# Splitting the tail of one store per block into 120 rows and 8 rows

## The chip, the cores and the metric

The kernel runs on one core of a Trainium2 chip. The metric is the device time of one execution in microseconds (us); a time is the median of several runs. Inside the core, TensorE (PE) multiplies matrices and writes to PSUM, VectorE (DVE), ScalarE (ACT) and GpSimd (POOL) work elementwise, and SyncE (SP) only issues transfers. Sixteen DMA engines move data between SBUF, the core's working memory of 128 partitions ("rows" below), and DRAM.

## The reference

The input is x with B = 4096 samples, F = 32 fields and D = 64 numbers per field, and one 64x64 matrix W[p] for each of the P = 32*31/2 = 496 pairs of fields (i, j) with i < j:

```python
idx_i, idx_j = np.triu_indices(F, k=1)
vi = inputs[:, idx_i, :]
vj = inputs[:, idx_j, :]
vidots = jnp.einsum('bpd,pde->bpe', vi, W)
return vidots * vj          # (4096, 496, 64) float32
```

The output has 4096*496*64 floats, 520 MB. All is float32. One pair of one sample is 64 floats, 256 bytes.

## The kernel before

A block is 256 samples: two tiles (`kt` = 0, 1) of 128 samples, one sample per partition. The 16 blocks are worked one after the other, and in each tile the 496 pairs go in five groups with 90, 106, 90, 105 and 105 pairs. A group fills one output buffer `ot` and leaves with one store, so there are ten stores in a block and 160 in all. Three `ot` buffers take turns.

```python
P = 128
NB = 2
groups = [(0, 3), (3, 7), (7, 11), (11, 17), (17, F - 1)]
cap = max(p0[b] - p0[a] for a, b in groups)
...
opool = ctx.enter_context(tc.tile_pool(name="opool", bufs=3))
psum = ctx.enter_context(tc.tile_pool(name="psum", bufs=4, space=bass.MemoryType.PSUM))
...
# the matrices W, 128 pairs to a load (112 in the last), one pair's 16 KB to a partition
nc.sync.dma_start(out=raw[c][: b - a, :], in_=wflat[a:b])
...
for s in range(NBLK * NB * NS):
    ...                                  # x of the next block is loaded from ACT's queue
    if pa == base:
        ot = opool.tile([P, cap, D], F32, tag="ot", name=f"ot_{t}_{g}")
    ...                                  # matmuls: x_i^T W into ps, up to 16 pairs
    if i in aside and c0 == 0:
        nc.scalar.copy(tmp, src)         # PSUM to SBUF
        nc.gpsimd.tensor_mul(dst, tmp, xj)
    else:
        nc.vector.tensor_mul(dst, src, xj)
    if pa + m == end:
        nc.sync.dma_start(
            out=rows_of(out, blk).rearrange("(p k) n d -> p k n d", k=NB)[:, kt, base:end, :],
            in_=ot[:, : end - base, :],
        )
```

Each store reads 128 rows of `ot`. A row is one piece of 90, 105 or 106 pairs, that is 23,040, 26,880 or 27,136 bytes without a gap, both in SBUF and in DRAM.

Of the kernel before, what the change touches and what calls it, by code (L numbers as in the profile page):

```python
# [12 lines left out]
def kernel(  # L13
# [16 lines left out]
    nc = tc.nc  # L30

    B, F, D = x.shape
    P = 128
    NB = 2
# [11 lines left out]
    cap = max(p0[b] - p0[a] for a, b in groups)  # L46

    aside = (1, 3, 5, 7, 9, 11, 13)

    cuts = [*range(0, NP, P), NP]  # L50
    wrows = list(zip(cuts[:-1], cuts[1:]))
# [13 lines left out]
    def rows_of(dram: bass.AP, blk: int) -> bass.AP:  # L65
        return dram[blk * NB * P : (blk + 1) * NB * P]

    def new_x(blk: int):

        xs[blk] = xpool.tile([P, 1 + NB * F, D], F32, tag="xs", name=f"xs_{blk}")  # L70
        nc.gpsimd.memset(xs[blk][:, 0, :], 0.0)  # L71

    def load_x(blk: int, eng, k0: int = 0, k1: int = NB):
        src = rows_of(x, blk).rearrange("(p k) f d -> p (k f) d", k=NB)
        eng.dma_start(out=xs[blk][:, 1 + k0 * F : 1 + k1 * F, :], in_=src[:, k0 * F : k1 * F, :])
# [7 lines left out]
    def load_w(c: int):  # L83

        a, b = wrows[c]
        pool, tag = ((opool, "ot"), (xpool, "xs"), (const, "w3"), (xpool, "xs"))[c]
        raw[c] = pool.tile([P, D * D], F32, tag=tag, name=f"raw_{c}")
        nc.sync.dma_start(out=raw[c][: b - a, :], in_=wflat[a:b])

    def order_w(c: int, k: int, copy):  # L90
        r = wrows[c][1] - wrows[c][0]
        rp = tpool.tile([P, EU, 2, D], F32, tag="tmp", name=f"rp_{c}_{k}")
        src = raw[c][:r, :].rearrange("p (d h e) -> p e h d", h=2, d=D)
        copy(rp[:r], src[:, k * EU : (k + 1) * EU])  # L94
        return rp

    def turn_w(c: int, k: int, rp, copy):
        r = wrows[c][1] - wrows[c][0]
        if c not in wT:
            wT[c] = const.tile([P, r, E2], F32, tag=f"w{c}", name=f"wT_{c}")  # L100
        pt = psum.tile([P, EU, P], F32, tag="ps", name=f"ptw_{c}_{k}")
        for n in range(EU):
            nc.tensor.transpose(  # L103
                pt[:, n, :r], rp[:r, n].rearrange("p h d -> p (h d)"), ident[:r, :r]
            )
        copy(wT[c][:, :, k * EU : (k + 1) * EU], pt[:, :, :r].rearrange("p e r -> p r e"))  # L106

    def turn_x(blk: int, k: int, q: int, copy):

        pt = psum.tile([P, RUN, P], F32, tag="ps", name=f"ptx_{blk}_{k}_{q}")  # L110
        for n in range(RUN):
            s = k * F + q * RUN + n
            nc.tensor.transpose(  # L113
                pt[:, n, :], xs[blk][:, s : s + 2, :].rearrange("p f d -> p (f d)"), ident
            )
        xT = xtpool.tile([P, RUN, P], F32, tag="xT", name=f"xT_{blk}_{k}_{q}")
        copy(xT, pt)  # L117
        return xT
# [32 lines left out]
    v, p, a = nc.vector.tensor_copy, nc.gpsimd.tensor_copy, nc.scalar.copy  # L151
# [10 lines left out]
    ot = None  # L162
    for s in range(NBLK * NB * NS):
        t, st = divmod(s, NS)
        blk, kt = divmod(t, NB)
        g, i, c0, m = steps[st]
        if st == LATE and kt == 0 and blk and blk + 1 < NBLK:
            new_x(blk + 1)
            load_x(blk + 1, nc.scalar)
        for what, *args in due.get(s, ()):  # L170
            if what == "x":
                xT[tuple(args)] = turn_x(*args, a)
            else:
                c, k = args
                turn_w(c, k, order_w(c, k, (v, p)[k % 2]), a)
                if k == NU - 1 and c == 1:
                    load_w(3)
                if k == NU - 1 and c == 3:
                    new_x(1)
                    load_x(1, nc.scalar)  # L180

        base, end = p0[groups[g][0]], p0[groups[g][1]]
        pa = p0[i] + c0
        if pa == base:
            ot = opool.tile([P, cap, D], F32, tag="ot", name=f"ot_{t}_{g}")
        ps = psum.tile([P, 2, CH, E2], F32, tag="ps", name=f"ps_{s}")
        for c, (lo, hi) in enumerate(wrows):
            lo, hi = max(pa, lo), min(pa + m, hi)
            if lo < hi:
                for h in range(2):  # L190
                    n = i + 1 - h
                    nc.tensor.matmul(  # L192
                        ps[:, h, lo - pa : hi - pa, :],
                        xT[blk, kt, n // RUN][h * D : (h + 1) * D, n % RUN, :],
                        wT[c][h * D : (h + 1) * D, lo - wrows[c][0] : hi - wrows[c][0], :],
                        start=True,
                        stop=True,
                    )
        o = pa - base
        j = 1 + kt * F + i + 1 + c0  # L200
        dst = ot[:, o : o + m, :].rearrange("p m (h e) -> p m h e", h=2)
        src = ps[:, :, :m, :].rearrange("p h m e -> p m h e")
        xj = xs[blk][:, j : j + m, :].rearrange("p m (h e) -> p m h e", h=2)
        if i in aside and c0 == 0:
            tmp = tpool.tile([P, CH, 2, E2], F32, tag="tmp", name=f"tmp_{s}")
            nc.scalar.copy(tmp, src)  # L206
            nc.gpsimd.tensor_mul(dst, tmp, xj)  # L207
        else:
            nc.vector.tensor_mul(dst, src, xj)  # L209
        if pa + m == end:  # L210
            nc.sync.dma_start(  # L211
                out=rows_of(out, blk).rearrange("(p k) n d -> p k n d", k=NB)[:, kt, base:end, :],
                in_=ot[:, : end - base, :],
            )


# [25 lines left out]
```

## Time and profile before

| what | value |
|---|---|
| time, median of 3 runs | 1359.63 us (1359.32 to 1359.97) |
| span of the profiled execution | 1357.5 us |
| PE busy | 1171.5 us (86%) |
| DVE busy | 951.3 us (70%) |
| POOL busy | 546.2 us (40%) |
| ACT busy | 371.1 us (27%) |
| DRAM read, written | 41.68 MB, 520.09 MB |
| mean rate of all transfers | 415 GB/s |
| from issue to landing of a store, min/median/max | 9.2/17.0/20.4 us |

Busy shares are averages over the span. In the profile's lists a group of instructions or a wait is named by its line in the kernel, its engine and the tiles that it writes and reads: `out_dram<-ot` is a store, `ps` a product in PSUM. A wait line such as "DVE ot L209 <- DMA out_dram<-ot" gives the total, the number and the longest of VectorE's waits that a landed store ended. A stage line gives a stretch of time, its length, the busy time of PE, PE's weight loads, DVE, ACT and POOL, then the granted TensorE clock, the mean busy share of the 16 DMA engines and the rate in GB/s. DMA queue lines give packets, MB and the share of 16 engines' time; q1 carries what SP issues, q10 what ACT issues, q8 and q14 fetch instructions.

### The profile page before, as it was taken

The page shows a single profiled execution, that of the slowest core. Times are in us where ns is not written, and L with a number is a line of the kernel's source. Part 1 is how long each engine was busy: PE and PEld are TensorE (multiplying, and loading weights), DVE is VectorE, ACT ScalarE, POOL GpSimd, SP SyncE. Part 2 cuts the span into 40 slices and gives each one's busy share as a digit, 9 for nine tenths or more (in the row PEclk, how much of TensorE's full clock was granted, in tenths as well). Part 3 has the DMA queues.
Part 4 walks back from the last instruction along what each step waited for, and adds up shares of the span by engine and source line. Part 5 has one row for each costly group of instructions (what it writes and reads, how often), then busy time and mean ns, then how long its engine had stood idle before and what let it go on. Part 6 is the DMA issues. An engine that isn't in the chain of part 4 may idle for free.

```text
span 1357.5 us, 17867 instructions
## 1 busy us (share of the span) xinstructions
PE 1171.5 (86%) x7424; PEld 681.2 (50%) x7424; DVE 951.3 (70%) x1259; ACT 371.1 (27%) x367; POOL 546.2 (40%) x253
## 2 busy tenths in 40 slices
PE   5998988888888888988889888899888889888894
PEld 4554554545455454554545445455454545545552
DVE  5686876767677676766667767677776777767783
ACT  3432322222222222222322222222222322223220
POOL 4544433443333443334434334433344433444441
PEclk9998998989999999998989999999898999999997
DMA  7999999999999999999999999999999999999997
GB/s 291 388 430 431 426 424 431 431 422 426 401 424 413 430 423 412 428 409 431 410 417 425 413 433 407 421 423 410 428 412 424 426 409 424 406 431 428 417 419 335
DMA packets 26128, 562.92 MB, mean 415 GB/s; under 512 B 2896, under 2 KB 2896, under 8 KB 2896
## 3 DMA queue, kind: packets, MB, share of 16 engines
q1 hardware_dynamic: 23744, 529.28, 92.0%
q10 hardware_dynamic: 2304, 32.51, 5.7%
q8 instruction: 58, 0.95, 0.3%
q14 instruction: 22, 0.18, 0.0%
HBM read 41.68 MB, written 520.09 MB: 414 GB/s over the span
## 4 chain that ended last, share of the span: by engine, by line
DMA 50%; PE 23%; DVE 18%; POOL 4%; issue 3%; ACT 0%; DVEq 0%; SPq 0%; POOLq 0%; ACTq 0%
DMA out_dram<-ot 49%; PE ps L192 19%; DVE ot L209 18%; PE ptx L113 4%; POOL ot L207 3%; DMA raw<-in_L_rec_W_dram 1%; POOL rp L94 1%; PE ptw L103 0%; ACT tmp L206 0%; DVE rp L94 0%; DVEq L209 0%; DVE xT L117 0%; ACT wT L106 0%; SPq L211 0%; POOLq L207 0%
## 5 line engine op out<-in xcount | busy, mean ns | idle before, releaser
L209 DVE TENSOR_TENSOR ot<-ps,xs 128x1024 f32<-128x1024 f32 (+15 forms) x1248 | 938.6, 807 | 378.4 <-DMA out_dram<-ot 195.3
L192 PE MATMUL ps<-wT,xT 64*128 64x512 f32 (+14 forms) x6272 | 1025.2, 467 | 118.0 <-DVE ot L209 105.5
L192 PEld LDWEIGHTS ps<-wT,xT 64*128 64x128 f32 x6272 | 554.0, 193 | 554.6 <-DVE ot L209 281.9
L207 POOL TENSOR_TENSOR ot<-tmp,xs 128x1024 f32<-128x1024 f32 x224 | 527.3, 2360 | 623.5 <-ACT tmp L206 397.7
L206 ACT COPY tmp<-ps 128x1024 f32<-128x1024 f32 x224 | 226.7, 1012 | 465.5 <-PE ps L192 460.6
L117 ACT COPY xT<-ptx 128x1024 f32<-128x1024 f32 x127 | 128.5, 1012 | 470.2 <-PE ptx L113 470.2
L113 PE MATMUL ptx<-ident,xs 128*128 128x128 f32 x1024 | 143.8, 285 | 48.9 <-DVE ot L209 34.3
L113 PEld LDWEIGHTS ptx<-ident,xs 128*128 128x128 f32 x1024 | 113.2, 144 | 95.4 <-issue 51.3
L71 POOL MEMSET xs<- 128x64 f32 x16 | 2.4, 151 | 146.7 <-DVE ot L209 146.7
L94 POOL COPY rp<-raw 128x1024 f32<-128x1024 f32 (+1 forms) x7 | 16.1, 2299 | 16.1 <-DMA raw<-in_L_rec_W_dram 11.8
L106 ACT COPY wT<-ptw 128x1024 f32<-128x1024 f32 (+1 forms) x15 | 14.7, 984 | 28.1 <-PE ptw L103 28.1
L103 PE MATMUL ptw<-ident,rp 128*128 128x128 f32 (+1 forms) x128 | 17.0, 280 | 3.2 <-DVE rp L94 2.0
L94 DVE COPY rp<-raw 128x1024 f32<-128x1024 f32 (+1 forms) x9 | 11.0, 1233 | 12.3 <-DMA raw<-in_L_rec_W_dram 11.9
L103 PEld LDWEIGHTS ptw<-ident,rp 128*128 128x128 f32 (+1 forms) x128 | 14.1, 145 | 10.2 <-issue 5.6
L106 ACT ACT_TABLE_LOAD x1 | 1.3, 1283 | 1.2 <-PEq L229 1.2
L117 DVE COPY xT<-ptx 128x1024 f32<-128x1024 f32 x1 | 1.2, 1208 | 0.0
L106 DVE COPY wT<-ptw 128x1024 f32<-128x1024 f32 x1 | 1.2, 1208 | 0.0
masks.py:197 POOL MEMSET ident<- 128x128 f32 x1 | 0.2, 205 | 0.3 <-POOLq L229 0.3
masks.py:199 POOL TENSOR_SCALAR_AFFINE_SELECT ident<-ident 128x128 f32<-128x128 f32 x1 | 0.3, 292 | 0.0
L229 POOL MEMSET const-float32-0.0<- 128x1 f32 x1 | 0.1, 98 | 0.2 <-issue 0.2
L229 POOL MEMSET const-bfloat16-1.0<- 128x1 bf16 x1 | 0.1, 101 | 0.0
L229 POOL MEMSET const-uint8-127<- 128x1 uint8 x1 | 0.1, 101 | 0.0
(1 smaller groups left out, 0.1 us busy)
## 6 DMA issues: line engine op xcount, KB each, us to landing
out_dram<-ot SPq DMA_DIRECT2D x64, 3360.0 KB, 16.2
out_dram<-ot SPq DMA_DIRECT2D x64, 2880.0 KB, 16.7
out_dram<-ot SPq DMA_DIRECT2D x32, 3392.0 KB, 17.2
xs<-in_r_inputs_dram ACTq DMA_DIRECT2D x15, 2048.0 KB, 16.6
raw<-in_L_rec_W_dram SPq DMA_DIRECT2D x3, 2048.0 KB, 15.6
raw<-in_L_rec_W_dram SPq DMA_DIRECT2D x1, 1792.0 KB, 15.7
xs<-in_r_inputs_dram ACTq DMA_DIRECT2D x1, 1024.0 KB, 11.4
xs<-in_r_inputs_dram SPq DMA_DIRECT2D x1, 1024.0 KB, 17.7
```

Source lines behind the costliest of these rows:

```text
L71: nc.gpsimd.memset(xs[blk][:, 0, :], 0.0)
L94: copy(rp[:r], src[:, k * EU : (k + 1) * EU])
L103: nc.tensor.transpose(pt[:, n, :r], rp[:r, n].rearrange("p h d -> p (h d)"), ident[:r, :r])
L106: copy(wT[c][:, :, k * EU : (k + 1) * EU], pt[:, :, :r].rearrange("p e r -> p r e"))
L113: nc.tensor.transpose(pt[:, n, :], xs[blk][:, s : s + 2, :].rearrange("p f d -> p (f d)"), ident)
L117: copy(xT, pt)
L192: nc.tensor.matmul(ps[:, h, lo - pa : hi - pa, :], xT[blk, kt, n // RUN][h * D : (h + 1) * D, n % RUN, :], wT[c][h * D : (h + 1) * D, lo - ...
L206: nc.scalar.copy(tmp, src)
L207: nc.gpsimd.tensor_mul(dst, tmp, xj)
L209: nc.vector.tensor_mul(dst, src, xj)
L229: nc = _bacc.Bacc("TRN2", target_bir_lowering=False, num_devices=1)
```

## The change

One store in ten, that of the third group (`g == 2`, 90 pairs) of a block's first tile (`kt == 0`), is cut in three. The first 62 pairs go out as before from all 128 rows. The last 28 pairs go out from rows 0 to 119 in one transfer and from rows 120 to 127 in another. Nothing else differs: the same bytes leave in the same order of groups, and all three transfers are issued by SP one after the other. The purpose is to move a little of the work of storing from some of the 16 DMA engines to others, because a transfer of 120 rows is not divided among them as one of 128 rows is.

```diff
     aside = (1, 3, 5, 7, 9, 11, 13)
+
+    SHIFT = 28
...
         if pa + m == end:
-            nc.sync.dma_start(
-                out=rows_of(out, blk).rearrange("(p k) n d -> p k n d", k=NB)[:, kt, base:end, :],
-                in_=ot[:, : end - base, :],
-            )
+            dst = rows_of(out, blk).rearrange("(p k) n d -> p k n d", k=NB)[:, kt]
+            cut = end - SHIFT if kt == 0 and g == 2 else end
+            parts = [(0, P, base, cut)]
+            if cut < end:
+                parts += [(0, P - P // 16, cut, end), (P - P // 16, P, cut, end)]
+            for r0, r1, n0, n1 in parts:
+                nc.sync.dma_start(
+                    out=dst[r0:r1, n0:n1, :], in_=ot[r0:r1, n0 - base : n1 - base, :]
+                )
```

## The prediction

> **What bounds the kernel now.** I read the page's slices and queues first, then waits, stages, and last the packet and landing records of the trace. The slices and queues of the page:
>
> ```profile
> DMA  7999999999999999999999999999999999999997
> GB/s 291 388 430 431 426 424 431 431 422 426 401 424 413 430 423 412 428 409 431 410 417 425 413 433 407 421 423 410 428 412 424 426 409 424 406 431 428 417 419 335
> ...
> q1 hardware_dynamic: 23744, 529.28, 92.0%
> q10 hardware_dynamic: 2304, 32.51, 5.7%
> q8 instruction: 58, 0.95, 0.3%
> ```
>
> The 16 DMA engines are busy from the second slice to the last but one: 92.0% of their time is stores and W loads (q1), 5.7% x loads (q10). No compute engine is that full (page: PE 86%, DVE 70%). The list of waits over the whole span says what compute is held by:
>
> ```profile
> DVE ot L209 <- DMA out_dram<-ot: 195.3, 97, 5.2
> POOL ot L207 <- DMA out_dram<-ot: 169.5, 73, 5.6
> DVE ot L209 <- PE ps L192: 156.9, 212, 2.7
> ```
>
> VectorE and GpSimd wait for an old store to land before they may refill one of the three `ot` buffers, so a store counts when its last engine is done. The stage view, one line per block of two tiles (ten stores each) in the steady part:
>
> ```profile
> 526.41:609.02 82.61, 71.34 (x460) 41.06 (x458) 58.64 (x78) 22.26 (x23) 33.12 (x15) 0.98 0.99 419
> 609.02:692.21 83.19, 73.69 (x460) 42.50 (x458) 58.64 (x78) 22.27 (x23) 33.10 (x15) 0.94 0.99 417
> 692.21:774.25 82.04, 72.18 (x460) 41.45 (x458) 58.73 (x78) 22.27 (x23) 33.10 (x15) 0.96 0.99 422
> ...
> sum 496.64, PE 434.72 PEld 250.97 DVE 351.80 ACT 133.59 POOL 198.66; mean PE 72.45 PEld 41.83 DVE 58.63 ACT 22.26 POOL 33.11
> ```
>
> A block takes 496.64/6 = 82.77 us, with PE busy 72.45 and DMA 0.99.
>
> The trace's landing records (16 per store, one per engine) show that this 0.99 hides an imbalance. Of the 16 the last is one engine alone: in the store issued at 817.83 the 8th lands 9.84 us after issue, the 15th 10.90, the 16th 15.73; in the last store 9.39, 10.92 and 14.39. This lag grows by some 0.3 us a store from about 138 us and stands at 5 to 6 us after about 300. The packet records say why: the lagging engine's 26,880-byte packets take 1011 to 1075 ns, the others' mostly 996; its 23,040-byte packets about 890 against 855. That is 34 ns in 1000, or 80 x 0.034 = 2.7 us a block.
>
> How much do the other engines idle for it? Counting running packets moment by moment in the six blocks gives 7.94 us of idle, averaged over 16 engines: 1.32 us a block, so 1.41 for each of the other 15. Between 120 and 300 us the same count is 0.33 us in 180: there all 16 are full.
>
> [...] The trace of before has 16 equal shares in all its transfers, and no transfer on fewer engines. [...] the trace shows one slow engine, without its number. [...] the last W load has 112 rows. The stage view over five microseconds of it (39 to 44) and five of the 128-row loads (9 to 14):
>
> ```profile
> 39.00:44.00 5.00, 4.68 (x32) 3.13 (x33) 2.37 (x3) 3.04 (x3) 4.07 (x3) 1.00 1.00 272
> 9.00:14.00 5.00, 1.78 (x9) 1.81 (x10) 2.07 (x2) 0.00 (x0) 2.04 (x1) 1.00 0.99 421
> ```
>
> At the same full DMA share (last column but one) the 112-row load moves 272 GB/s against 421: its 16 KB packets take 933 ns on average after the first round, the others' 611. [...]
>
> **The change part by part.** Its order of instructions differs from before only in the stores: 16 more 120-row and 16 more 8-row issues, and different semaphore numbers.
>
> *Removed from the one engine that 120 rows leave out.* Packet times in the trace lie on a line: 8,192 bytes 309 ns, 16,384 bytes 611, 23,040 bytes 855, 26,880 bytes 996, so 0.0367 ns a byte plus 9 ns. Its eight packets shrink from 90 pairs (23,040 bytes, 855 ns) to 62 pairs (15,872 bytes, about 592 ns): 8 x 263 = 2.1 us a block, 34 us in 16 blocks. If this is the slow engine, it goes from 82.77 to 80.6 us a block.
>
> *Added to the others.* Engines 0 to 14 move the same bytes in 16 packets instead of 8: 8 x 9 ns = 0.07 us. Engines 0 to 7 take one 7,168-byte packet more: 9 + 263 = 0.27 us, 0.35 in all. Busy now 82.77 - 1.41 = 81.36, they go to 81.4 (8 to 14) and 81.7 (0 to 7).
>
> [...] Engines 0 to 7 would stand at 81.7 + 2.18 + 0.82 = 84.7 us a block, above the slow engine's old 82.77.
>
> *Issue.* SP issues two more transfers a block at 332 ns (median of its store issues); it waits for VectorE nearly all the time (1271.9 us), so this costs nothing.
>
> **How it could go.**
>
> *A. [...]* The other 15 set the time. Their work ended before at 1359.6, less their idle after 300 us (1.41 x 12.6 blocks = 17.8), less the 5.0 us by which their half landed before the last store's end: 1336.8. Add 0.35 x 16 = 5.6, and 1 to 2 for idle that stays: about 1343, 1.2% faster. More than 2% (below 1332.4) is hardly to be had: it would need the other engines' work to shrink. For A speak the size, 28 pairs, which fits the measured 2.7 us of excess, and the lag that is always one engine's.
>
> *B. [...]* 1336.8 + 16 x (0.35 + 3.0) = 1390 if fully so, 1364 at half. For it speaks the 112-row load at 272 GB/s. Against it: that was a load, [...] more than half of the 15 land within about 0.2 us of each other, a few 1 to 2 us later.
>
> *C. The slow engine is another one than the one left out* (7, say). Then it gets 0.35 us more a block, 5 us in all: 1365, or as far as 1390 and over with B.
>
> *D. Compute becomes the bound.* PE has 10.3 us of slack in 82.77 and the gain is 1 to 2 us a block; this takes nothing from A.
>
> **Range and chances.** I give A 0.47, B 0.45 and C 0.08. A lies around 1343, B around 1375, so a point between the two is the honest middle: 1350. The range 1336 to 1386 takes in nearly all of A and most of B. Over 2% faster needs more than A has: 0.03. Over 2% slower (above 1386.8) is the upper third of B and a part of C: 0.15. Within 2%: 0.82.
>
> **What the changed profile would show.** The q1 packets rise by 16 x 128 data packets and 16 x 23 semaphore writes to 26,160 if k is 15 and 8. Under A the 7,168-byte packets take about 272 ns, the last landing comes nearer to the others than 5 us, GB/s in the steady stages goes from 419 to about 425, and the DVE and POOL waits for stores (195.3 and 169.5 us) shrink. Under B these packets take 400 to 550 ns in the 120-row transfers and about 1 us in the 8-row ones, and the steady stages fall below 419 GB/s with the DMA share still at 0.99. Under C the lag of the last engine stays at 5 to 6 us or grows. The prediction is wrong if the time falls below 1336, which would mean that the others' work was not the limit I took it for, or above 1386, where collisions would reach transfers next to the split ones.

## The result, and the profile after

The changed kernel takes 1401.16 us against 1359.68 (medians of four runs each): 3.2% slower (ratio 1.0317, 95% interval 1.0281 to 1.0353). The prediction had 1350 us and a range of 1336 to 1386. The sign and the range were both missed.

The page of the changed kernel, its slices and its queues:

```profile
DMA  7999999999999999999999999999999999999997
GB/s 293 363 429 423 423 422 414 421 416 420 413 395 401 411 412 412 396 400 398 412 409 412 385 410 403 411 408 394 412 405 413 403 398 406 392 411 418 407 401 333
DMA packets 28546, 562.93 MB, mean 403 GB/s; under 512 B 3264, under 2 KB 3264, under 8 KB 5312
...
q1 hardware_dynamic: 26160, 529.28, 91.1%
```

The DMA engines look as busy as before in the digits, yet the rate has fallen from 415 to 403 GB/s. The 26,160 packets of q1 are those that the prediction counted for 15 engines in the 120-row piece and 8 in the 8-row piece. The packets under 512 B, taken as one for each engine of a transfer (2896 for the 181 transfers before, 16 to each), rose to 3264, by 23 for each of the 16 split stores. So the number of engines in each piece is the one it assumed.

The list of waits of the changed kernel (total us, times, longest):

```profile
DVE ot L211 <- DMA out_dram<-ot: 261.6, 116, 7.2
...
POOL ot L209 <- DMA out_dram<-ot: 214.3, 71, 7.1
...
DVE ot L211 <- PE ps L194: 143.3, 203, 3.2
```

Both waits for a landed store grew, VectorE's from 195.3 to 261.6 us and GpSimd's from 169.5 to 214.3. VectorE's wait for PE fell a little. The stores hold everything back more than before.

The stage view of the changed kernel, in stretches of about one block (columns as before):

```profile
452.04:537.00 84.96, 71.49 (x458) 40.59 (x456) 58.38 (x78) 21.93 (x23) 33.11 (x15) 0.98 0.98 407
537.00:623.00 86.00, 72.14 (x462) 41.07 (x460) 58.85 (x79) 22.58 (x23) 33.13 (x15) 0.98 0.97 404
...
881.00:967.00 86.00, 73.98 (x463) 41.77 (x462) 59.13 (x79) 22.80 (x23) 33.17 (x16) 0.96 0.98 406
sum 514.96, PE 439.98 PEld 248.96 DVE 351.86 ACT 133.67 POOL 198.67; mean PE 73.33 PEld 41.49 DVE 58.64 ACT 22.28 POOL 33.11
```

Six blocks take 514.96 us, 85.83 each instead of about 82.7. PE and DVE work as long as before. The DMA share went from 0.99 to 0.97 or 0.98: the engines idle more, not less. Counted moment by moment in the packet records, from 526 to 1023 us, the mean engine idles about 15 us of 497, where it idled about 8 before. A change made to even out the 16 engines made them more uneven.

The landing records show how. This is the split store issued at 727.85 us, each engine's landing after the issue of the piece, in order:

```
62 pairs, 128 rows: 9.62 9.63 9.66 9.67 9.68 9.70 9.76 9.76 10.02 10.03 10.59 10.77 11.70 13.85 15.72 16.36
28 pairs, 120 rows (issued 0.93 us later): 10.87 10.88 11.49 11.49 11.66 11.85 12.08 12.48 12.58 12.69 12.77 13.50 17.16 18.98 19.58
28 pairs,   8 rows (issued 1.65 us later): 10.43 11.22 11.36 11.66 12.00 12.17 12.34 18.59
```

Where the kernel before had one late engine there are three here, and all three take part in the 120-row piece, so none is the one that it leaves out. The latest takes 4.15 us from one landing to the next for eight 7,168-byte packets, which at 272 ns each would be 2.18.

### The profile page after: what moved, and what is told of

Read it like the earlier page. It is cut to its first block, busy times and chain, and to the rows that moved or that the text cites. A ratio compares the mean times of both kernels' runs of the same rounds, so it can differ in the third digit from the quotient of the medians.

```text
span 1398.2 us, 17946 instructions
## 1 busy us (share of the span) xinstructions
PE 1181.8 (85%) x7424; PEld 677.1 (48%) x7424; DVE 952.6 (68%) x1259; ACT 371.4 (27%) x367; POOL 546.0 (39%) x253
## 2 busy tenths in 40 slices
DMA packets 28546, 562.93 MB, mean 403 GB/s; under 512 B 3264, under 2 KB 3264, under 8 KB 5312
## 3 DMA queue, kind: packets, MB, share of 16 engines
q1 hardware_dynamic: 26160, 529.28, 91.1%
## 4 chain that ended last, share of the span: by engine, by line
DMA 59%; PE 19%; DVE 17%; issue 2%; POOL 1%; DVEq 0%; ACT 0%; SPq 0%; POOLq 0%
DMA out_dram<-ot 58%; DVE ot L211 17%; PE ps L194 15%; PE ptx L115 3%; DMA xs<-in_r_inputs_dram 1%; PE ptw L105 1%; POOL rp L96 1%; POOL ot L209 1%; DVEq L211 0%; DVE rp L96 0%; ACT tmp L208 0%; ACT wT L108 0%; SPq L219 0%; DVEq L245 0%; POOLq L96 0%
## 5 line engine op out<-in xcount | busy, mean ns | idle before, releaser
L211 DVE TENSOR_TENSOR ot<-ps,xs 128x1024 f32<-128x1024 f32 (+15 forms) x1248 | 938.5, 808 | 417.0 <-DMA out_dram<-ot 261.6
L194 PE MATMUL ps<-wT,xT 64*128 64x512 f32 (+14 forms) x6272 | 1035.8, 469 | 149.4 <-DVE ot L211 136.7
```

What stands on the lines that cost most here:

```text
L194: nc.tensor.matmul(ps[:, h, lo - pa : hi - pa, :], xT[blk, kt, n // RUN][h * D : (h + 1) * D, n % RUN, :], wT[c][h * D : (h + 1) * D, lo - ...
```

## Experiments

The theories at this point: (1), the prediction's rival B: the packets of the uneven pieces collide; (2) the cost is that of more transfers and smaller packets. "Collide" says no more here than that packets of several engines, running at the same time, take longer than the same packets undisturbed. How much longer (twice the time in the pieces of 120 and of 64 rows, four times in 8 adjacent rows) was the author's assumption, which no trace of before shows. Beside them stands the question which engine was the slow one. Each timed kernel was run in rounds with the kernel before on the same chip; the experiments are spread over three chips.

### The cut alone: both pieces from 128 rows

```diff
-                parts += [(0, P - P // 16, cut, end), (P - P // 16, P, cut, end)]
+                parts += [(0, P, cut, end)]
```

> The same store is cut at the same 28 pairs, but both pieces go out from all 128 rows. Theory 1 [...]: nothing collides here, so the time is that of the kernel before plus eight 9 ns packets a block, 1359 to 1363 us, and the 7,168-byte packets stay at 272 ns. Theory 2 (the cost lies in more transfers, smaller packets and one more landing to wait for): about half of the 41 us or more stays, 1375 us or above.

Measured: 1360.79 us against 1359.89, ratio 1.0003 (0.9994 to 1.0011). The 7,168-byte packets take 272 ns at the median, 273 on average between 526 and 1023 us. The waits for a landed store stay well below those of the changed kernel (261.6 and 214.3 us):

```profile
DVE ot L211 <- DMA out_dram<-ot: 203.4, 99, 5.7
POOL ot L209 <- DMA out_dram<-ot: 186.9, 75, 15.4
```

Small packets and a second landing cost 0.9 us, which the noise covers. Theory 2 falls, as far as two transfers in place of one go.

### No engine left out: rows 0-63 and rows 64-127

```diff
-                parts += [(0, P - P // 16, cut, end), (P - P // 16, P, cut, end)]
+                parts += [(0, P // 2, cut, end), (P // 2, P, cut, end)]
```

> The last 28 pairs go out as rows 0 to 63 and rows 64 to 127. Each piece is spread over all 16 engines with 4 rows each, so no engine gets less or more than before. Theory 1 [...] 4.35 us instead of 2.18 a block on every engine; with lagging engines and their victims on top 1390 to 1410 us, and many 7,168-byte packets near 540 ns. Rival (the loss of the changed kernel comes from its uneven division among the engines, 15 and 8 of them[...]): 1359 to 1364 us.

Measured: 1403.44 us, ratio 1.0326 (1.0258 to 1.0394). All 16 engines take part in each piece (between 526 and 1023 us 76 transfers have 1215 packets under 512 B, 16 to each but for one) and the loss is still that of the changed kernel. The waits of this kernel are nearly the changed kernel's too:

```profile
DVE ot L211 <- DMA out_dram<-ot: 260.7, 121, 6.6
POOL ot L209 <- DMA out_dram<-ot: 213.5, 69, 6.6
```

So what costs is which rows a transfer takes at a time, not the uneven division. In each of the blocks 3 to 11 (counted from 0) the 7,168-byte packets average 372 to 485 ns, and the slowest tenth takes over 565 ns to 1.05 us.

### Which engine is slow: a ruler of row counts

```diff
+            probe = kt == 0 and g == 2 and 5 <= blk <= 12
+            k = blk - 4
+            cut = end - 1 if probe else end
+            parts = [(0, P, base, cut)]
+            if probe:
+                parts += [(0, k, cut, end), (k, 16, cut, end), (16, P, cut, end)]
```

> In blocks 5 to 12 the last pair of one store goes out as k rows, 16-k rows and 112 rows, k from 1 to 8. [...] the landing records of the pieces tell which engine is the slow one: the smallest number of rows at which the last landing is some 5 us late is its number plus one. If the slow engine is number 15, none of the pieces with 1 to 15 rows has a late landing. If it is another one, as the changed kernel's three late engines in its 120-row transfers suggest, the pieces are late from some number of rows on. Time: within 1355 to 1375 us.

Measured: 1360.88 us, and the last landing of each small piece, as its distance behind the landing before it:

```
rows in the piece          1     2     3     4     5     6     7     8     9    10    11    12    13    14    15
last behind last but one   -   0.49  0.22  0.01  6.16  4.74  4.11  5.26  4.12  4.40  6.13  4.24  4.05  3.20  4.04   (us)
```

(The piece of 1 row landed with the early engines.) From 5 rows on, a landing is 3 to 6 us late, with fewer it never is. So row counts take the late engine in from the fifth row on and keep it. An engine's number here is its place in this order, counted from 0, for the records carry none: the slow engine of the kernel before is number 4. A piece of 8 rows holds it (5.26 us), and so does one of 15 (4.04). The 120-row piece has 15 landings too and the 8-row piece of the change 8; that they take engines 0 to 14 and 0 to 7, as the prediction has it, was the author's assumption. By it the change relieved number 15, which is not the late one.

### Twice the pairs, and half

```diff
-    SHIFT = 28
+    SHIFT = 56        # and, in another kernel, 14
```

> As the changed kernel, with 56 pairs instead of 28 in the pieces of 120 and 8 rows. Theory 1 [...]: the loss grows with the bytes that go out in the uneven pieces, 1430 to 1450 us. Theory 2 (a fixed cost for each split store): as with 28 pairs, 1398 to 1408 us. Relief of the slow engine, were it number 15, would show as a loss that grows less than in proportion.

> The changed kernel with 14 pairs in the uneven pieces. The two sizes measured so far (28 pairs: +41.5 us, 56 pairs: +98.8) lie on a line of 2.05 us a pair that meets zero at 8 pairs. If the other engines' idle time (1.3 us a block) pays for the first part of the collisions, 14 pairs lie on this line: +13 us, 1368 to 1376 us. If every collision counts in full, for instance because engine 4 takes part in each, they cost in proportion to 28 pairs: +21 us, 1378 to 1384 us.

Measured: with 56 pairs 1458.68 us, ratio 1.0728 (1.0684 to 1.0773); with 14 pairs 1370.21 us, 1.0079 (1.0048 to 1.0109), beside 1359.77. So 14, 28 and 56 pairs cost 10.4, 41.5 and 98.8 us. That is not in proportion. The line through the two larger sizes gives 12.8 at 14 pairs, near to what was measured. This fits the reading that the first part of the collisions is paid from idle time (1.41 us a block before). The loss with 56 pairs ran over the upper end of what was expected. With 56 pairs GpSimd's wait for stores is the larger of the two:

```profile
POOL ot L209 <- DMA out_dram<-ot: 351.1, 79, 18.2
DVE ot L211 <- DMA out_dram<-ot: 321.1, 128, 6.8
```

### The rows of a transfer by themselves

Only the last store is changed, into 48 transfers of 8 rows, one row an engine (between 1367 and 1376 us 104 packets of data stand beside 112 under 512 B; a transfer has 8 of each).

```diff
+            if last:
+                a1, a2 = base + 33, base + 67
+                parts = [(slice(r, r + 8), base, a1) for r in range(0, P, 8)]
+                parts += [(slice(r, P, 16), a1, a2) for r in range(16)]
+                parts += [(slice(q + r, q + r + 29, 4), a2, end) for q in range(0, P, 32) for r in range(4)]
```

> Only the very last store (105 pairs) is changed: it goes out in 48 transfers of 8 rows, each spread over 8 engines with one row an engine, in three geometries told apart by packet size: 33 pairs (8,448 bytes) of 8 adjacent rows, 34 pairs (8,704 bytes) of rows 16 apart, 38 pairs (9,728 bytes) of rows 4 apart. A packet alone takes 319, 329 and 366 ns by the line of the kernel before. Theory 1 [...]: adjacent rows [...] about 4 times 310, 1.2 us; rows 16 apart [...] about 650 ns; rows 4 apart [...] about 366 ns. Rival (few rows, or few engines, are slow in themselves): the three sizes take about the same time per byte. The whole time is some 20 to 60 us longer, which says nothing.

Measured (1380.01 us in all, where the tail counts for nothing), from the packet records:

```
rows               bytes   shortest   median   mean   longest (ns)   mean / shortest
adjacent            8448        319      319    603      2711            1.9
16 apart            8704        328      504    500       689            1.5
4 apart             9728        366      369    370       374            1.01
```

The order is the expected one, and rows 4 apart do not disturb each other (mean 370 ns, shortest 366). The factors 4 and 2 behind the other two expected times did not come out. The first packets of adjacent rows take 1179, 1087, 1124, 986 and 1307 ns, near four times 310. Later ones often take 319 ns; why is not shown. The longest packets of adjacent rows (2242 to 2711 ns) run beside the tail of the store before; the 76 that start after 1350.5 us, when it has landed, average 518 ns, 1.6 times the shortest. Rows that lie otherwise in SBUF also go to other addresses in DRAM, and no run separates the two. What the packets collide at is not shown. The stage view of the three phases of this kernel shows the same in its last two columns (DMA share, GB/s):

```profile
1346.00:1354.00 8.00, 0.00 (x0) 0.00 (x0) 0.00 (x0) 0.00 (x0) 0.00 (x0) 0.50 0.33 65
1358.00:1365.00 7.00, 0.00 (x0) 0.00 (x0) 0.00 (x0) 0.00 (x0) 0.00 (x0) 0.50 0.45 119
1367.00:1376.00 9.00, 0.00 (x0) 0.00 (x0) 0.00 (x0) 0.00 (x0) 0.00 (x0) 0.50 0.27 112
```

A busy engine moves 65 / (0.33 x 16) = 12.3 GB/s with adjacent rows, 16.5 with rows 16 apart, 25.9 with rows 4 apart. The 8-row piece of the change has adjacent rows.

### Does engine 4 set the time of the kernel before?

```diff
+            if kt == 0 and g == 3:
+                spare = nc.dram_tensor(f"spare_{blk}", (KX, end - base, D), F32, kind="Internal").ap()
+                nc.sync.dma_start(out=spare, in_=ot[0 : 4 * KX - 3 : 4, : end - base, :])
```

with KX = 4 in one kernel and 5 in the other, otherwise the kernel before. The rows lie 4 apart, as those that ran undisturbed in the last store (370 ns against 366).

> The kernel before with an extra store once in a block: rows 0, 4, 8 and 12 of the 105 pairs of one store go a second time to a spare buffer in DRAM. Four rows use engines 0 to 3[...]; each of the four engines gets 0.996 us more a block. If engine 4 alone sets the time and the others idle 1.4 us a block, this is nearly hidden: 1359 to 1364 us.

> The same extra store with five rows (0, 4, 8, 12 and 16), so that engine 4 takes part. If engine 4 alone sets the time, all of its 1.03 us a block is paid: 16 x 1.03 = 16.5 us, 1373 to 1379 us. Rival (no single engine sets the time, or it is not number 4): as with four rows, within 2 us of that run.

Measured: four rows 1360.63 us, ratio 1.0006 (0.9993 to 1.002); five rows 1376.39 us, 1.0114 (1.0096 to 1.0132), beside 1359.91. One row more, on one engine more, costs 15.8 us; 16 x 1.03 is 16.5. Work for engines 0 to 3 costs 0.7 us, which the noise covers; work for number 4 is paid nearly in full. The waits, first with four rows, then with five:

```profile
DVE ot L211 <- DMA out_dram<-ot: 201.1, 101, 6.2
POOL ot L209 <- DMA out_dram<-ot: 174.4, 75, 5.6
```

```profile
DVE ot L211 <- DMA out_dram<-ot: 217.3, 100, 5.3
POOL ot L209 <- DMA out_dram<-ot: 190.6, 72, 5.6
```

With five rows each of the two waits is 16 us longer, as much as the medians differ. (The profiled execution with four rows was a long one, 1366.08 us. What it lost lies in its first 60 us, which moved 296 GB/s against 329 with five rows.)

### Is it the addresses in DRAM?

```diff
-        src = rows_of(x, blk).rearrange("(p k) f d -> p (k f) d", k=NB)
+        src = rows_of(x, blk).rearrange("(k p) f d -> p k f d", k=NB)
...
-                out=rows_of(out, blk).rearrange("(p k) n d -> p k n d", k=NB)[:, kt, base:end, :],
+                out=rows_of(out, blk).rearrange("(k p) n d -> p k n d", k=NB)[:, kt, base:end, :],
```

> The kernel before with the samples of a block dealt to the partitions in another order: partition p holds samples p and 128+p instead of 2p and 2p+1, so every engine writes to other addresses in DRAM while it reads the same partitions. If the slowness of engine 4 comes from the DRAM addresses that its rows go to, the lag of one engine goes away or changes, and the time may fall by up to 20 us, to 1340 to 1355 us. If it belongs to the engine or its partitions, the lag stays at 5 to 6 us and the time at 1355 to 1365 us.

Measured: 1360.94 us, ratio 1.0009 (0.9996 to 1.0021). The store that lands around 828 us has its first 15 engines between 828.30 and 829.96 and the last at 834.25. The lag stays, so this order of addresses is not its cause. Why engine 4 is slow stays open; no run here separates the engine from the rows that it reads in a full store.

### Which engines are late in the changed kernel?

The ruler, put into the changed kernel: once in the third store of the block's second tile (the first line below) and once, in another kernel, in the store after the split one.

```diff
+            if kt == 1 and g == 2 and 5 <= blk <= 12:      # the other kernel: kt == 0 and g == 3
+                k, cut = blk - 4, end - 1
+                parts = [(0, P, base, cut), (0, k, cut, end), (k, 16, cut, end), (16, P, cut, end)]
```

> The changed kernel, and in blocks 5 to 12 the last pair of the second tile's third store goes out as k rows, 16-k rows and 112 rows. The landing records of the pieces number its late engines. If the slow engine of the kernel before (number 4 by the ruler in that kernel) is the one that the split transfers hit hardest, the pieces of 5 and more rows are late and those of 4 and fewer are not; the other late engines come in between 8 and 14, since only one of the eight landings of the 8-row transfers was late. Number 15 is late in none. Time 1398 to 1408 us.

> The changed kernel with the ruler (k, 16-k and 112 rows of one pair) in the store that follows the split one, where its trace has three late engines. The pieces' landings number them: by the 8-row landings one of them is among 0 to 7 (number 4 if the slow engine of before is still behind), two are among 8 to 14, one of these number 9, the one left late half a block later. Number 15 is in none. Time 1398 to 1412 us.

Measured: 1405.59 and 1409.14 us. In the first kernel the pieces of up to 9 rows have no late landing and those of 10 to 15 do: the late engine is number 9. In the second the pieces of up to 6 rows have none and those of 7 and more do: number 6. Both times one landing alone is late, all eight blocks agree with one number, and neither number is 4. Both expectations failed on number 4, the second also on three late engines. Number 15 is not it, for the 15-row piece, which leaves 15 out, takes in the late one. The two kernels ran on different chips (the one that gave number 4 ran on a third, and the extra store that confirms number 4 on the chip that gave number 9), so program and chip are not separated as what decides between 9 and 6. That the collisions choose the engine is an inference, and what picks the one is open.

### The 120-row piece alone

```diff
-                parts += [(0, P - P // 16, cut, end), (P - P // 16, P, cut, end)]
+                parts += [(0, P - P // 16, cut, end)]
```

This leaves 28 pairs of rows 120 to 127 of one store in ten unstored, 0.9 MB of 520.

> The changed kernel without the piece of 8 rows: the last 28 pairs of rows 120 to 127 are not stored in one store of ten, which leaves out 0.9 of 520 MB. If engines 0 to 7 set the time, as the sum of the prediction had it, the piece's 1.09 us a block is saved: 16 x 1.09 = 17 us, 1380 to 1387 us. If the 120-row piece and an engine beyond 7 (number 9) set it, little changes: 1394 to 1402 us.

Measured: 1401.58 us, ratio 1.0291 (1.0252 to 1.0329), against the changed kernel's 1.0317 (1.0281 to 1.0353). The 8-row piece costs nothing that can be told apart: the two intervals leave it between some -4 and +11 us, less than the 17 expected. With the 120-row piece alone the whole loss is there.

## Why the prediction was wrong

**The path.** Following the last landing from store to store gives the time of the engine that is late, which is not always the same one in the changed kernel. The excess over what its packets cost at the usual rate, averaged over ten blocks (4 to 13), in us a block:

```
                                            before   after   without the 8-row piece
eight (after: seven) plain stores            2.18     1.30     0.86
the split store: 62-pair piece                 -      0.90     0.85
the split store: 120-row piece                 -      1.86     2.09
two stores beside the x load                 5.41     6.54     6.77
sum                                          7.60    10.61    10.56
```

(The first row of "before" holds the third store, 0.24, which is the split one after.) The x load itself is 8 x 0.611 = 4.9 of the fourth row. The difference of 3.0 us a block is the loss: 16 x 3.0 = 48, less what the first blocks do not pay, against 41.5 measured. With both pieces from 128 rows the 62-pair piece has an excess of about 0.1 and the second piece next to none.

**What was right.** The bound (the last engine of each store), the number of engines used by 120 and 8 rows, the packet count, the 272 ns of a packet of 7,168 bytes that nothing disturbs, the issue that costs nothing. Rival B was right that the packets of the split store slow one another (those of 7,168 bytes average 387 ns between 526 and 1023 us, against 273 with both pieces from 128 rows), and its main term was of the right size: the 120-row piece was put at +2.18 us, by the author's assumption that its packets take twice 272 ns, and the late engine pays 1.86 to 2.09.

**Step 1 that failed: "If this is the slow engine".** The relief of 2.1 us went to number 15, and the late engine is number 4. I gave A 0.47 because 28 pairs fit the 2.7 us of excess and because the lag is always one engine's. Neither says which engine. That it was number 15 was a guess, and the rulers found 4, 9 and 6. The trace of before could not tell the number, since every transfer in it uses all 16 engines (2896 packets under 512 B for 181 transfers). The ruler tells it for about 1 us of run time. What came is C together with B, for which the prediction had "as far as 1390 and over", but C had a chance of only 0.08. Even with number 15 slow, A would by these numbers have failed, since the 120-row piece costs late engines about the 2 us which the relief brings; this is an estimate and was not tried.

**Step 2: the sum of B, 1390 if fully so.** It adds 3.35 us a block to 81.36 and gets 84.7; the stage view has 85.83. Its terms were partly the wrong ones. The 8-row piece was put at +0.82 us above the bare time on engines 0 to 7, by the author's assumption that its packets take four times 272 ns; nothing of it can be told apart in the run without it. The landings of the changed kernel fit this. In blocks 3 to 8 (counted from 0) the last 120-row landing comes after every 8-row landing (748.36 against 748.09 us in block 8), so the latest engine is none of 0 to 7, if an engine takes its pieces in order. From block 9 on an 8-row landing is the last, but only 0.26 to 0.37 us behind the last 120-row one, about the bare 0.27. Two terms were missing. The 62-pair piece, itself of 128 rows, is slowed by 0.90 us on the late engine. In the packet records single 15,872-byte packets take up to 2.15 us instead of 592 ns while other engines are already in the 120-row piece. The author's reading is that those slow the late engine's packets; no run shows it apart. That collisions reach neighbours was named at the end of the prediction as what would break its range, and not counted. The two stores beside the x load grew by 1.1 us. They grew by nearly the same with 14 pairs (1.1) and with 56 (1.4), so most of this does not follow the size of the pieces. It may be work that the late engine has and number 4 has not: in the kernel before, those 16 KB instruction fetches that start at 621.6, 718.6 and 784.0 us, for example, are each followed by one landing that lags 0.9 to 1.3 us more than in the store before. No run tests this.

**Step 3: engines that are out of step.** The prediction held it against B that a few of the 15 engines land 1 to 2 us after the others; that this keeps them from colliding was an assumption. For the early engines it holds in part: the ninth of 16 engines pays only 1.0 us in the 120-row piece. A late engine does not escape. When it comes to its 120-row piece the others are already in the next store. In the split store issued at 727.85 us the late engines' packets cluster around 535 ns, twice 272. So being out of step did not protect the late engines here.

**The idle time.** The prediction took 1.41 us a block of idle as what the change could win. It was rather the cushion that hid the first collisions, which fits that 14 pairs cost 10.4 us, a quarter of what 28 do.

## What to carry to other kernels

Here, cutting a store by columns cost nothing that the noise does not cover (ratio 1.0003), and cutting 28 pairs of one store in ten by rows cost 3%. Packets of 7,168 bytes took 273 ns on average in pieces of 128 rows, 387 ns in those of 120 and 8 rows and 372 to 485 ns in halves of 64; packets of 8 adjacent rows averaged 1.9 times their shortest, those of 8 rows 4 apart 1.01 times. Before work is moved from a slow engine, find its number (small pieces of k rows, read at their landings), and measure whether the packets of the new pieces keep their time. A mean DMA share of 0.99 can hide one engine that sets the time, and work added to engines below it may cost next to nothing (0.7 us of 1360 here).

## What was not expected of the hardware

- One DMA engine, number 4, takes about 34 ns more in 1000 on the packets of stores, and shows no such delay in the first three W loads (of their 384 packets of 16 KB 358 take 611 to 613 ns, and only one 620 to 650). The one other order of DRAM addresses that was tried did not matter to it. It was number 4 on two chips. The cause is open.
- Under collisions another engine fell behind (number 9 in one run, number 6 in another), and within each of the two all eight blocks agree on it, while in the changed kernel's own trace the latest engine of the split store changes at block 9. After 300 us the latest engine takes about the usual time in plain stores: 8.03 us for eight 27,136-byte packets (median), where the slow engine of before took 8.33.
- Half-row stores (64 and 64 rows) of 28 pairs cost as much as the 120 + 8 cut, 3.3% of the kernel, with all 16 engines in each piece.

No version that beats the kernel before came out of this. Of the pieces of 1 to 15 rows in the ruler only those of 4 rows and fewer left out number 4; moving part of its work to engines 0 to 3 was not tried.
